# A second level of the block scheme in a graph layer's adjacency product

## The chip, the cores and the metric

One core of a Trainium2 chip runs the whole program. The metric is the time of one execution on the device in microseconds (us). TensorE (PE) multiplies matrices, VectorE (DVE), ScalarE (ACT) and GpSimd (POOL) work on elements, SyncE (SP) issues the DMAs.

## The reference

Two residual graph layers over 16 batches of 1024 nodes with 512 features, all in f32:

```python
h = jnp.maximum(_layernorm(x), 0.0)
y = jnp.einsum('nm,bmd->bnd', adj, h)
x = x + jnp.einsum('bnd,do->bno', y, weight) + bias          # layer 0
h = jnp.maximum(_layernorm(x), 0.0)
x = x + gnn_attention(h, W, a, beta, adj)                    # layer 1
```

Layer 1 forms logits from `h`, multiplies them by `adj`, takes a softmax over the nodes, multiplies it by `h W`, adds `beta` times `h W`, and applies ELU.

## The kernel before

**Products.** Every product of matrices is cut in two by two blocks and done with seven block products instead of eight (the Strassen scheme in Winograd's form). The table `PRODUCTS` names them in order: p1, p2, p6, p5, p7, p3, p4. The left factor's blocks are A11, A12, A21, A22 and the sums S1 to S4, the right factor's B11 to B22 and T1 to T4. Four blocks of sums C11, C12, C21, C22 and again S1, S2, S4 come out, since they are at once the left factor of the next product.

**Layer 0, one batch.** `layer0_a` multiplies the transposed `h` by the transposed adjacency (A in what follows); `layer0_b` multiplies the result by the weight (B). A block product of A is two halves p of 128 features, each of four matmuls over k (K 128, 512 moving columns), in one PSUM bank. Banks are named by kind: Y is shared by p1, p6, p7 and p4 and accumulates over them, X by p5 and p3, W is p2's. After each half, ACT copies the bank out or DVE adds it to a C block, which takes the partial sum before the next product accumulates in the same bank. A block product of B is two halves q of four matmuls with 256 columns; after each, DVE adds the bank to the residual tile `xr` (`done` in `layer0_b`).

**Work beside it.** `products_a` and `products_b` call `after(n)` behind each half, so that a batch has 14 numbered steps in A and 14 in B. Plans, which are dictionaries from step to calls, say what is issued there. Every engine runs its instructions in the order in which they are recorded. In A of batch b lie the rest of batch b-1 (`plan_out`): the store `keep` of `xr` to DRAM, its layer norm statistics (`bn_stats` and `bn_aggr` on DVE, then the power -0.5 on POOL), the Relu on ACT into tiles `u` of their own, two passes for the attention logits on DVE for each chunk of 128 nodes (`logits`), sums of `u` for layer 1 (`sums`) and their stores (`store`); the loads of the residual x into `xr` (`load_res`, four DMAs for each of the four tiles) and, on them, the bias (`add_bias`; POOL, on DVE for the first batch). Also there and in B lies the layer norm of batch b+1 (`plan_norm_a`, `plan_norm_b`: `load_x`, `h_stats`, `h_relu`, `h_sums`). The first softmax of layer 1 lies beside the last batch (`FIRST_A`, `FIRST_B`).

```python
for p in range(2):                      # products_a, one block product
    for k in range(HC):
        pe.matmul(ps, a_blk(an, k)[:, ts(p, P)], b_blk(bn, k), ...)
    ...                                 # read by ACT or DVE
    after(2 * n + p)
```

**Buffers.** Pool `xp` has four tiles, one for each `xr`; `up` has seven, `b4` twelve, `b2` five, PSUM eight banks.

All instructions are recorded through the helper `InOrder`, so the profile gives line 109 for all of them; they are told apart by tile names (`y_` for A, `po_` for B of layer 0, `z_` and `pq_` in layer 1).

Of the kernel before, what the change touches and what calls it, by code (L numbers as in the profile page):

```python
# [59 lines left out]
def kernel(  # L60
# [57 lines left out]

    def products_a(name, a_blk, b_blk, after):


        c = new_c(name)
        s = {}
        banks = {}
        for n, (prod, an, bn, kind, first, last) in enumerate(PRODUCTS):
            for p in range(2):
                if first:
                    banks[kind, p] = bank(f"{name}_{kind}{p}")
                ps = banks[kind, p]
                for k in range(HC):  # L130
                    pe.matmul(
                        ps, a_blk(an, k)[:, ts(p, P)], b_blk(bn, k),
                        start=(first and k == 0), stop=(last and k == HC - 1),
                        skip_group_check=True,
                    )
                c11, c12, c21, c22 = (c[k][:, p, :] for k in ("C11", "C12", "C21", "C22"))
                if prod == "p1":
                    act.copy(c11, ps)
                elif prod == "p2":
                    add(c11, ps, c11)  # L140
                elif prod == "p6":
                    act.copy(c12, ps)
                elif prod == "p5":
                    act.copy(c22, ps)
                elif prod == "p7":
                    add(c22, ps, c22)
                elif prod == "p3":
                    if not s:
                        for k in ("S1", "S2", "S4"):
                            s[k] = b4.tile([P, 2, 512], F32, tag="b4", name=f"{name}_{k}")  # L150
                    s1, s2 = s["S1"][:, p, :], s["S2"][:, p, :]
                    add(c12, ps, c12)
                    add(s1, c12, c22)
                    add(s2, s1, c11, ALU.subtract)
                    add(c12, c11, c12, ALU.subtract)
                else:
                    act.copy(c21, ps)
                    add(s["S4"][:, p, :], c21, s["S2"][:, p, :], ALU.subtract)
                after(2 * n + p)
        return {  # L160
            "A11": c["C11"], "A12": c["C21"], "S3": c["C12"], "A22": c["C22"],
            "S1": s["S1"], "S2": s["S2"], "S4": s["S4"],
        }
# [47 lines left out]

    def inv_std(r, nb, mv):

        k = r.shape[1]
        pool.tensor_scalar(r, mv[:, :, 1], EPS, 1.0, op0=ALU.add, op1=ALU.mult)
        pool.tensor_tensor(r, r, half[:, 0:k], op=ALU.pow)
        pool.tensor_scalar(nb, mv[:, :, 0], -1.0, 1.0, op0=ALU.mult, op1=ALU.mult)
        pool.tensor_tensor(nb, nb, r, op=ALU.mult)
# [6 lines left out]
    class Norm:  # L225


        def __init__(self, name, src, dst):
            self.name, self.src, self.dst = name, src, dst
            self.n = src.shape[1]  # L230

        def stats(self):
            mv = stat.tile([P, self.n, 2], F32, tag="mv", name=f"mv_{self.name}")
            for k in range(self.n):
                stats(mv[:, k, :], self.src[:, k, :])
            self.r = stat.tile([P, self.n], F32, tag="r", name=f"r_{self.name}", bufs=3)
            self.nb = stat.tile([P, self.n], F32, tag="nb", name=f"nb_{self.name}", bufs=3)
            inv_std(self.r, self.nb, mv)

        def relu(self, c=slice(None)):  # L240
            for k in range(self.n):
                act.activation(
                    self.dst[:, k, c], self.src[:, k, c], AF.Relu,
                    scale=self.r[:, k : k + 1], bias=self.nb[:, k : k + 1],
                )

# [14 lines left out]
    def h_stats(b, k):  # L261

        if k % 2 == 0:
            hs[b, k // 2] = b8.tile([P, HC, D], F32, tag="b8", name=f"h_{b}_{k // 2}")
        dst = hs[b, k // 2][:, ts(k % 2, 2), :]
        h_norms[b, k] = Norm(f"h{b}_{k}", xs.pop((b, k)), dst)
        h_norms[b, k].stats()
# [4 lines left out]
    def left_half(k, a11, a12, a21, a22, s):  # L272

        s1, s2, s4 = (s[n][:, ts(k, 2), :] for n in ("S1", "S2", "S4"))
        add(s1, a21, a22)
        add(s2, s1, a11, ALU.subtract)
        add(a21, a11, a21, ALU.subtract)
        add(s4, a12, s2, ALU.subtract)
# [41 lines left out]
    def add_bias(b, nh, q):  # L320

        t = xrs[b, nh, q]
        bias = bias_bc[:, None, :].to_broadcast([P, 2, D])
        (pool if b else dve).tensor_tensor(t, t, bias, op=ALU.add)
# [18 lines left out]
    class LayerOut:  # L343
# [18 lines left out]
        def stats(self, nh, q):  # L362
            xr = xrs.pop((self.b, nh, q))
# [5 lines left out]
            self.us[nh, q] = up.tile([P, 2, D], F32, tag="up", name=f"u_{self.b}_{nh}_{q}")  # L369
            self.norms[nh, q] = Norm(f"u{self.b}_{nh}_{q}", xr, self.us[nh, q])  # L370
            self.norms[nh, q].stats()

        def relu(self, nh, q):
            self.norms[nh, q].relu()

        def logits(self, nh, q):
            junk = self.s["S1"].rearrange("p k d -> p (k d)")[:, 0:D]
            for k in range(2):
                self.logit_parts(4 * nh + 2 * q + k, self.us[nh, q][:, k, :], junk, v_bcs)
# [8 lines left out]
        def sums(self, q):  # L388
            u1, u2 = self.us[0, q], self.us[1, q]
            left_half(q, u1[:, :, 0:HD], u2[:, :, 0:HD], u1[:, :, HD:D], u2[:, :, HD:D], self.s)  # L390
# [382 lines left out]
    def logit_weights(k):  # L773

        v = stat.tile([P, DC], F32, tag="v", name=f"v_{k}")
        junk = up.tile([P, D], F32, tag="up", name=f"junk_{k}")
        for dc in range(DC):
            dve.tensor_tensor_reduce(
                out=junk, in0=w1_t[:, dc, :], in1=v_bcs[k], scale=1.0, scalar=0.0,
# [34 lines left out]
    def plan_first():  # L814
# [4 lines left out]
            12: [(add_bias, 0, 0, 0)], 13: [(add_bias, 0, 0, 1)],  # L819
        }  # L820

    def plan_out(o, b):

        plan = {
            -1: [(o.keep, 0, 0), (o.stats, 0, 0), (o.keep, 0, 1), (o.stats, 0, 1)],
            0: [(o.relu, 0, 0), (o.keep, 1, 0), (o.stats, 1, 0)],
            1: [(o.relu, 0, 1), (o.keep, 1, 1), (o.stats, 1, 1)],
            2: [(o.relu, 1, 0)], 3: [(o.relu, 1, 1)],
        }

        for i, (nh, q) in enumerate(halves):
            plan.setdefault((4 if b == 1 else 2) + i, []).append((o.logits, nh, q))
        for q in range(2):
            plan.setdefault((8 if b == 1 else 6) + q, []).extend([(o.sums, q), (o.store, q)])
        for i, (nh, q) in enumerate(halves):
            plan.setdefault(3 + i, []).append((load_res, b, nh, q))
            plan.setdefault(6 + i, []).append((add_bias, b, nh, q))
        return plan

    def plan_norm_a(b):  # L840
        return {
            8: [(h_stats, b, 0), (h_stats, b, 1)],
            9: [(h_relu, b, 0), (h_relu, b, 1), (load_x, b, 2), (load_x, b, 3)],
            12: [(h_stats, b, 2)], 13: [(h_stats, b, 3), (h_relu, b, 2)],
        }

    def plan_norm_b(b):
        plan = {0: [(h_relu, b, 3)], 2: [(h_sums, b, 0)], 5: [(h_sums, b, 1)]}
        if b + 1 < B:
            plan[7] = [(load_x, b + 1, 0), (load_x, b + 1, 1)]  # L850
        return plan

    def plan_softmax(order, s):
# [33 lines left out]
        -1: "R0 R1 R2 R3", 2: "B E0", 3: "E1 R4", 4: "E2 R5", 5: "E3 R6 S", 6: "b E4 R7",  # L887
        7: "E5", 8: "E6", 9: "E7 s", 10: "D", 12: "T1a", 13: "T1b",
    }
    FIRST_B = {0: "d", 1: "T2a", 2: "T2b", 4: "T3a", 5: "T3b"}  # L890
# [3 lines left out]
    sms = [Softmax(b) for b in range(B)]  # L894
    for b in range(B):
        plans = [plan_first() if b == 0 else plan_out(LayerOut(b - 1), b)]
        if b + 1 < B:
            plans.append(plan_norm_a(b + 1))
            if b == 1:
                plans.append({2: [(logit_weights_back, 0), (logit_weights_back, 1)]})  # L900
            plan_b = merged(plan_norm_b(b + 1), plan_softmax(EARLY_B.get(b, {}), sms[0]))
            if b == 0:
                plan_b = merged(
                    {2: [(add_bias, 0, 1, 0), (add_bias, 0, 1, 1)]}, plan_b,
                    {9: [(logit_weights, 0)], 11: [(logit_weights, 1)]},
                )
        else:
            plans.insert(0, plan_softmax(FIRST_A, sms[0]))
            plans.append({
                8: [(load_u, 0, ("U00", "U01"))],  # L910
                10: [(load_u, 0, ("U10", "U11", "S2", "S1", "S4"))],
            })
            plan_b = merged(plan_softmax(FIRST_B, sms[0]), plan_softmax(LOGITS_B, sms[1]))
        if 0 < b <= G:
            plans.append({13: [(store_mask, b - 1)]})
        layer0_a(b, merged(*plans))
        layer0_b(b, plan_b)
# [69 lines left out]
```

## Time and profile before

| | |
|---|---|
| median of 8 runs | 2361.21 us (2357.83 to 2363.21) |
| the profiled execution | 2359.86 us, its span 2358.0 us |
| granted TensorE clock, mean | 0.997 |
| ACT busy in layer 1, 1200 to 1400 us | 135.5 us |
| ACT busy in layer 0, 600 to 800 us | 52.9 us |
| HBM | 251.92 MB read, 133.50 MB written |

The span runs from the first to the last instruction; the execution's own time has 1.9 us more around it. A busy time is the time in which an engine had an instruction under way. In a group's line stand the operation, the tile written and those read, the shapes and the count; then the total time, the mean of one in ns, and the idle time of the engine before them with what ended it. In a timeline's line stand start and length, and in brackets the idle time before.

### The profile page before, as it was taken

The page shows a single profiled execution, that of the slowest core. Times are in us where ns is not written, and L with a number is a line of the kernel's source. Part 1 is how long each engine was busy: PE and PEld are TensorE (multiplying, and loading weights), DVE is VectorE, ACT ScalarE, POOL GpSimd, SP SyncE. Part 2 cuts the span into 40 slices and gives each one's busy share as a digit, 9 for nine tenths or more (in the row PEclk, how much of TensorE's full clock was granted, in tenths as well). Part 3 has the DMA queues.
Part 4 walks back from the last instruction along what each step waited for, and adds up shares of the span by engine and source line. Part 5 has one row for each costly group of instructions (what it writes and reads, how often), then busy time and mean ns, then how long its engine had stood idle before and what let it go on. Part 6 is the DMA issues. An engine that isn't in the chain of part 4 may idle for free.

```text
span 2358.0 us, 26003 instructions
## 1 busy us (share of the span) xinstructions
PE 2334.3 (99%) x7264; PEld 1373.6 (58%) x7264; DVE 1862.7 (79%) x3950; ACT 1071.3 (45%) x2675; POOL 560.1 (24%) x732
## 2 busy tenths in 40 slices
PE   9999999999999999999999999999999999999998
PEld 5655556665566655666555666556665566655665
DVE  5888877788788888787968787877877778777774
ACT  3212212212222232222356776667766677666743
POOL 1223323223322233232102221122211222102220
PEclk9999999999999999999999999999999999999999
DMA  6444434434346445345554556555565554555541
GB/s 219 108 152 152 167 119 152 161 128 158 137 134 206 160 162 180 105 145 184 195 189 152 165 186 202 188 166 172 185 216 172 182 164 157 183 174 172 170 129 46
DMA packets 207234, 382.99 MB, mean 162 GB/s; under 512 B 80240, under 2 KB 88432, under 8 KB 207088
## 3 DMA queue, kind: packets, MB, share of 16 engines
q1 hardware_dynamic: 206768, 380.81, 49.0%
q8 instruction: 57, 0.93, 0.2%
q14 instruction: 89, 0.73, 0.1%
q10 hardware_dynamic: 320, 0.52, 0.1%
HBM read 251.92 MB, written 133.50 MB: 163 GB/s over the span
## 4 chain that ended last, share of the span: by engine, by line
PE 78%; DVE 7%; DMA 6%; ACT 5%; SPq 2%; issue 2%; POOL 0%; DVEq 0%; ACTq 0%
PE y_Y L109 17%; PE z_Y L109 13%; PE po_Y L109 9%; PE y_X L109 8%; PE pq_Y L109 6%; PE z_X L109 6%; PE po_X L109 5%; PE y_W L109 4%; PE z_W L109 4%; PE pq_X L109 3%; DMA md<-mx 2%; ACT e L109 2%; PE po_W L109 2%; PE pq_W L109 2%; DVE e L109 2%; SPq L109 2%
## 5 line engine op out<-in xcount | busy, mean ns | idle before, releaser
L109 POOL TENSOR_TENSOR x<-x,r 128x512 f32<-128x512 f32 x120 | 226.2, 1896 | 895.9 <-DVE x L109 486.2
L109 ACT ACTIVATE e<-e,nm 128x256 f32<-128x256 f32 x480 | 237.4, 498 | 159.6 <-DVE nm L109 159.6
L109 ACT COPY y_C<-y_Y 128x512 f32<-128x512 f32 x96 | 56.2, 586 | 547.0 <-PE y_Y L109 538.7
L109 DVE CUSTOM_DVE_ANT_0 e<-e,mask 128x256 f32<-128x256 f32 x512 | 234.4, 509 | 70.6 <-DMA mask<-maskd 37.6
L109 DVE CUSTOM_DVE_ANT_0 uS<-u,v_bc 128x512 f32<-128x512 f32 x240 | 241.8, 1008 | 19.5 <-DMA v_bc<-vd 3.1
L109 PE MATMUL y_Y<-adjT_B,h 128*128 128x512 f32 x512 | 226.7, 596 | 1.9 <-ACT adjT_B L109 1.9
L109 PE MATMUL z_Y<-pT,ul_U 128*128 128x512 f32 x512 | 224.9, 592 | 0.0
L109 ACT ACTIVATE e<-s2b,s1b 128x256 f32<-128x256 f32 x512 | 214.7, 506 | 16.5 <-DMA s2b<-s2d 16.5
L109 DVE STREAM_TRANSPOSE pT<-e 128x512 f32<-128x512 f32 x240 | 155.6, 686 | 70.6 <-ACT e L109 70.6
L109 ACT ACTIVATE h<-x,nb_h,r_h 128x512 f32<-128x512 f32 (+1 forms) x132 | 98.4, 793 | 219.3 <-POOL nb_h L109 219.1
L109 PE MATMUL pq_Y<-w_c,z_C 128*128 128x256 f32 x768 | 176.3, 381 | 1.7 <-DVE z L109 0.9
L109 PE MATMUL po_Y<-w_c,y_C 128*128 128x256 f32 x768 | 173.6, 379 | 0.0
L109 POOL TENSOR_TENSOR xr<-xr,bias_bc 128x1024 f32<-128x1024 f32 x60 | 151.6, 2535 | 66.0 <-DMA xr<-in_x_dram 49.4
L109 PEld LDWEIGHTS y_Y<-adjT_B,h 128*128 128x128 f32 x512 | 97.8, 191 | 118.8 <-issue 115.4
L109 PEld LDWEIGHTS z_Y<-pT,ul_U 128*128 128x128 f32 x512 | 97.3, 190 | 115.6 <-issue 111.9
L109 PEld LDWEIGHTS pq_Y<-w_c,z_C 128*128 128x128 f32 x768 | 144.4, 190 | 33.2 <-issue 7.7
L109 PEld LDWEIGHTS po_Y<-w_c,y_C 128*128 128x128 f32 x768 | 145.9, 190 | 26.7 <-issue 7.7
L109 ACT ACTIVATE r<-z,rs 128x256 f32<-128x256 f32 x192 | 95.7, 499 | 110.0 <-DVE z L109 110.0
L109 DVE TENSOR_TENSOR xr<-po_Y,xr 128x512 f32<-128x512 f32 x128 | 86.6, 687 | 55.2 <-PE po_Y L109 55.0
L109 PE MATMUL po_X<-w_c,y_S 128*128 128x256 f32 x512 | 115.7, 379 | 0.0
L109 PE MATMUL pq_X<-w_c,z_S 128*128 128x256 f32 x512 | 115.6, 379 | 0.0
L109 PE MATMUL z_Y<-pT_T,ul_U 128*128 128x512 f32 x256 | 112.5, 592 | 0.0
(127 smaller groups left out, 4164.9 us busy)
## 6 DMA issues: line engine op xcount, KB each, us to landing
mask<-maskd SPq DMA_DIRECT2D x128, 512.0 KB
x<-in_x_dram SPq DMA_DIRECT2D x64, 512.0 KB
xr<-in_x_dram SPq DMA_DIRECT2D x256, 128.0 KB
x1d<-xr SPq DMA_DIRECT2D x64, 512.0 KB
ul_U<-ud_U SPq DMA_DIRECT2D x64, 512.0 KB
x<-x1d SPq DMA_DIRECT2D x64, 512.0 KB
out_dram<-x SPq DMA_DIRECT2D x252, 128.0 KB
ud_U<-u SPq DMA_DIRECT2D x60, 512.0 KB
```

The source lines that it names most:

```text
L109: return lambda *args, **kwargs: tc.keep_in_program_order(f(*args, **kwargs))
```

## The change

For batches 1 to 15, A is done by `products_a2`. There p1, p5 and p3 are cut once more: the 256 by 512 left block and the 512 by 512 right block into two by two blocks, with seven inner products r1 to r7 of two matmuls each (128 stationary columns, 256 moving). r1, r6 and r7 accumulate in a bank y of their own; r1's value is copied out by ACT before r6 accumulates, r6's is read by DVE before r7 does. r4 and r2, r3 go to the halves of the product's two banks. DVE then adds the copied values to these banks in PSUM. The inner product steps alternate with the plain matmuls of p2, p6 and p7; p4 comes last. A has 25 numbered steps.

- `inner_right` makes the inner right sums of B11, T1 and B22 once, in batch 0, in place and in tiles `ext`, which take four tiles of `up` and one of `b2`. `inner_left` makes the left ones in each batch, four DVE adds for each product.
- The layer norm statistics of x for batches 1 to 15 and of `u` go from DVE to ACT, one chunk of 512 features at a call (`Norm.sums`): a pass with the total, a one-element operation for the mean, a pass with the squares.
- Relu writes `u` over `xr`. `load_res` of the next batch therefore waits for the store of `u`.
- `add_bias` is always on POOL, in halves of 256 columns, and lies in steps 0 to 7 of B.
- Logits, sums and statistics are issued by chunk or by pair of adds, at steps of their own. The chunks of the first `u` tile and one of the second lie in B. Steps in the first batch, whose A stays as it was, are scaled from 25 to 14. The softmax beside the last batch is spread further, into B.

```diff
     def products_a(name, a_blk, b_blk, after):
...
+    def products_a2(name, a_blk, b_blk, inner, after):
...
+            lefts = {
+                "r1": left[:, 0:2, P : 2 * P], "r2": left[:, 2:4, P : 2 * P],
+                "r7": left[:, 0:2, 0:P], "r4": left[:, 2:4, 0:P], "r5": sums[:, 0],
+                "r6": sums[:, 1], "r3": sums[:, 2],
+            }
...
+            outs = {
+                "r1": (y, True), "r4": (i0[:, 0:256], first), "r5": (x, not first),
+                "r6": (y, False), "r7": (y, False), "r2": (i1[:, 0:256], first),
+                "r3": (i1[:, 256:512], False),
+            }
+            def step(r):
+                o, start = outs[r]
+                for k in range(2):
                     pe.matmul(
+                        o, lefts[r][:, k, :], rights[r][:, k, :], start=(start and k == 0),
+                        stop=(k == 1), skip_group_check=True,
                     )
+                if r == "r1":
+                    act.copy(t[:, 0, :], y)
+                elif r == "r5":
+                    act.copy(t5, x)
+                elif r == "r6":
+                    add(t[:, 1, :], y, t5)
+                elif r == "r7":
+                    act.copy(t[:, 2, :], y)
+                    if first:
+                        i0v = i0.rearrange("p (a n) -> p a n", a=2)
+                        add(i0v, i0v, t[:, 2:3, :].to_broadcast([P, 2, 256]))
+                    else:
+                        add(t[:, 3, :], y, t5)
+                        add(i0, i0, t[:, 2:4, :].rearrange("p a n -> p (a n)"))
+                elif r == "r3":
+                    add(i1, i1, t[:, 0:2, :].rearrange("p a n -> p (a n)"))
+
+            return [partial(step, r) for r in ("r1", "r4", "r5", "r6", "r7", "r2", "r3")]
...
+        k = 0
+        for two, one in (("p1", "p2"), ("p5", "p6"), ("p3", "p7")):
+            inn, pla = inner_steps(two), plain_steps(one)
+            for m in range(7):
+                inn[m]()
+                pla[m if m < 4 else m + 1]()
+                if m == 3:
+                    pla[4]()
+                    if one != "p2":
+                        reads(one, 0)
+                elif m == 4:
+                    reads(two, 0)
+                    if one == "p2":
+                        reads(one, 0)
+                elif m == 6:
+                    for prod in (two, one) if one == "p2" else (one, two):
+                        reads(prod, 1)
+                after(k + m)
+            k += 7
...
+        def sums(self, k):
...
+            act.activation(junk, self.src[:, k, :], AF.Identity, accum_out=total)
+            act.activation(mean, total, AF.Copy, scale=-1.0 / D)
+            act.activation(junk, self.src[:, k, :], AF.Square, bias=mean, accum_out=var)
...
-        bias = bias_bc[:, None, :].to_broadcast([P, 2, D])
-        (pool if b else dve).tensor_tensor(t, t, bias, op=ALU.add)
+    def add_bias(b, nh, q, oh):
+
+        t = xrs[b, nh, q][:, :, ts(oh, HD)]
+        bias = bias_bc[:, None, ts(oh, HD)].to_broadcast([P, 2, HD])
+        pool.tensor_tensor(t, t, bias, op=ALU.add)
...
+        late = 4 if b == 1 else 0
+        return steps(
+            (-1, o.keep, 0, 1), (-1, o.keep, 1, 0), (-1, o.keep, 1, 1), (-1, o.stats, 0, 1, 1),
+            (0, o.stats, 1, 0, 0), (1, o.relu, 0, 0), (2, o.stats, 1, 0, 1),
+            (3, o.stats, 1, 1, 0), (4, o.relu, 1, 0), (5, o.stats, 1, 1, 1), (6, o.relu, 0, 1),
+            (8, o.relu, 1, 1),
+            (3 + late, o.logits, 0, 0, 0), (5 + late, o.logits, 0, 0, 1),
+            (7 + late, o.logits, 1, 0, 0), (8 + late, o.logits, 1, 0, 1),
+            (9 + late, o.sums, 0, 0), (10 + late, o.sums, 0, 1), (10 + late, o.store, 0),
+            (11 + late, o.logits, 0, 1, 0), (12 + late, o.logits, 0, 1, 1),
+            (12 + late, load_res, b, 0, 0), (13 + late, load_res, b, 1, 0),
+            (13 + late, o.logits, 1, 1, 0), (15 + late, o.logits, 1, 1, 1),
+            (16 + late, o.sums, 1, 0), (17 + late, o.sums, 1, 1), (17 + late, o.store, 1),
+            (19 + late, load_res, b, 0, 1), (20 + late, load_res, b, 1, 1),
+        )
...
+            (9, h_stats, b, 0, 0), (10, h_stats, b, 0, 1), (12, h_stats, b, 1, 0),
+            (13, h_stats, b, 1, 1), (14, h_relu, b, 0), (15, load_x, b, 2), (16, h_relu, b, 1),
+            (17, load_x, b, 3),
...
+                    (11, out_of.stats, 0, 0, 0), (12, out_of.stats, 0, 0, 1),
+                    (13, out_of.stats, 0, 1, 0), (12, out_of.keep, 0, 0),
```

## Prediction

> **What bounds the kernel now.** I read the page's engine shares first, then busy time in stretches, then the chain of waits in order of time, then groups by shape and the timelines of DVE, ACT, POOL and SP in one batch. All instructions carry L109, a recording helper, so I go by tiles.
>
> ```profile
> span 2358.0 us, 26003 instructions
> PE 2334.3 (99%) x7264; PEld 1373.6 (58%) x7264; DVE 1862.7 (79%) x3950; ACT 1071.3 (45%) x2675; POOL 560.1 (24%) x732
> ```
>
> PE is busy all the time. The two stretches below are one layer 0 batch: adjacency product (A), then weight product (B). Columns: length, then busy us of PE, PEld, DVE, ACT, POOL, granted clock, DMA share, GB/s.
>
> ```profile
> 532.00:580.10 48.10, 48.10 (x114) 21.47 (x113) 42.43 (x82) 12.89 (x19) 18.28 (x29) 1.00 0.48 164
> 580.10:604.30 24.20, 24.20 (x113) 21.13 (x112) 16.67 (x29) 3.62 (x5) 3.08 (x8) 1.00 0.25 88
> ```
>
> PE has no gap; DVE is 88% busy in A, ACT 27%. The chain of waits there is PE alone:
>
> ```profile
> 539.26 6.87 PE y_W L109 x16
> 580.46 3.45 PE po_Y L109 x16
> ```
>
> A product of A (8 matmuls, two records each) is 6.87 us, 0.859 per 512-column matmul; one of B (8 matmuls of 256 columns) is 3.45, 0.432 each. So time can be won only by taking matmul columns away, and lost by making PE wait.
>
> **What PE loses.** In 15 of 16 batches p1, p5 and p3 become seven inner products of two 256-column matmuls: 14 x 0.432 = 6.04 us for 6.87, so 0.83 a product, 45 x 0.83 = **37 us**. A falls from 48.1 to 45.6 us. Weight loads are nearly hidden at this shape already (PEld 21.1 of 24.2 in B).
>
> **What it asks of DVE in A.** A 512-element add is 0.69 us and a 1024-element one 1.22, so a 256-element one is about 0.42. New: 8 inner left sums and 4 inner adds (12 x 0.42 = 5.0) and 6 adds that read and write PSUM. No row writes PSUM from DVE; the nearest reads it (`xr<-po_Y`, 0.69), bounds 0.6 and 1.2, I take 0.69: 4.1. Kept: 14 reads of products at 0.66 = 9.2, 16 logit passes at 1.58 a pair = 12.6, 8 `u` sums = 5.3, small 0.4. Sum 36.6 of 45.6. Gone: 12 normalization statistics at 0.66 + 0.18, and the collisions with POOL's bias:
>
> ```profile
> 545.51 5.49 POOL L109 TENSOR_TENSOR xr<-xr,bias_bc 128x1024 f32<-128x1024 f32 x2 [0.68 <-DMA xr<-in_x_dram]
> 546.20 2.60 DVE L109 CUSTOM_DVE_ANT_0 uS<-u,v_bc 128x512 f32<-128x512 f32 x1
> 548.84 2.71 DVE L109 CUSTOM_DVE_ANT_0 uS<-u,v_bc 128x512 f32<-128x512 f32 x1
> ```
>
> A logit pass of 0.69 takes 2.6 beside a bias add; four bias adds a batch hold DVE about 8 us.
>
> **What it asks of ACT.** A chunk's statistics become three activations. The rows:
>
> ```profile
> L109 ACT ACTIVATE er<-er,nm 128x256 f32<-128x256 f32 x32 | 15.8, 499 | 2.4 <-DMA er<-ed 2.4
> L109 ACT ACTIVATION_READ_ACCUMULATOR e<-e,nm 128x1 f32 x480 | 91.2, 190 | 0.0
> L109 ACT ACTIVATE h<-x,nb_h,r_h 128x256 f32<-128x256 f32 x8 | 4.3, 594 | 2.5 <-POOL nb_h L109 2.5
> L109 ACT ACTIVATE h<-x,nb_h,r_h 128x512 f32<-128x512 f32 x124 | 94.2, 806 | 216.8 <-POOL nb_h L109 216.6
> ```
>
> 256 more elements cost 806 - 594 = 212 ns, a second per-partition operand 594 - 499 = 95. So the total pass (no such operand) is 499 - 95 + 212 = 0.62, the squares (one) 0.71, the one-element mean 0.19; consecutive accumulating passes start one duration apart, but the mean waits for the read-out, about 0.1, and two handoffs add 0.08: **1.7 us a chunk**. No row shows that dependent chain: without the waits 1.5, with every read-out and handoff in full 2.0. In A: 9 chunks 15.3, 6 pairs of Relu at 1.52 = 9.1, 8 copies of 0.59 = 4.7, 9 half copies at 0.37 = 3.3: 32.4 of 45.6. Neither engine is full; what counts is who is late in its queue.
>
> **Where PE can now wait.** Inner r6 accumulates where ACT must first have copied r1; r7 accumulates where DVE must first have added r6 and the ACT copy of r5. From r6's end to r7 lie only two plain matmuls, 1.72 us, of which 0.2 to reach DVE, 0.42 for the add and 0.15 back leave 0.95 for queueing. I lay the queues out from A's start, a step being 1.72 us (that with r6 2.58). ACT can begin the chunks of u(0,0) when DVE has finished its xr, 20.3 us into the B before, 3.9 ahead of A; that one and u(0,1) are four chunks of 1.7. First group: so ACT does them to 2.9, r1's copy to 3.3 (wanted 5.2), a chunk, two Relus, r5's copy at 6.8; DVE adds to 7.3, r7 is due 7.75: no wait. Then ACT: two chunks to 10.1, r7's copy, DVE's correction to 11.3, the read of C11 to 12.05, two Relus, a chunk to 15.2, the second read of C11 to 15.8. DVE, in order behind that read, adds W1 to 16.55, then four logit passes to 19.75 and two sums to 21.0, and only then r6's add of p5, to 21.4. r7 is due 20.65: PE waits **0.9 us**. Third group: the add is done at 33.3, r7 due 34.45: none. With 2.0 a chunk the same walk gives 1.1 + 0.75 + 1.2 = 3.05 us a batch, with 1.5 about 0.1. I take 0.9, the value of the rows: 15 x 0.9 = 13.5 us.
>
> **Moves with one answer.** The bias goes to B as eight halves (POOL's undisturbed add of 512, `x<-x,r` at 1340.82, takes 1.32): 10.6 us of POOL beside B's first half. DVE's adds there read PSUM; two of them, `z<-pq_Y` at 1395.01, take 1.28 together while POOL has an add under way, so I charge nothing. The bound above: each bias half holds DVE its 1.32 us; DVE's B (14 adds, 8 h sums, 4 inner sums) is 17 of 24.2, so 10.6 more would run some 3 us over, 45 us in all. In layer 0's first batch bias and statistics leave DVE and twelve right sums of 0.69 come, under 6.87 us products: hidden, 0 to 3. The Trainium skill, "GPSIMD Engine Reference", section "Key points", says that GpSimd contends with VectorE where the latter has two SBUF inputs. By that rule these adds go free; the trace has only the few rows above to say so.
>
> **Transfers.** U now overwrites xr in place, so the next residual waits for U's store. SP's order late in A: five stores and two small ones (before: 567.46 to 574.45, 7.0 us), one x load (3.1), then xr(0,1) (2.9), landing 2.4 later. The sums end at 35.7, so it lands near 51, 4.5 us into B; POOL's and DVE's next work waits there, and r_h and the Relu of the next h behind POOL. Y1 is wanted again 8.6 into B: hidden, 3.4 us to spare. In batch 1 everything is four steps later, 6.9 us: PE waits 2 to 4, I take 3 (0 to 6). In batch 15 softmax steps move into B: 1 (0 to 5).
>
> **Sum.** 2359.9 (the profiled execution, 1.3 under the median 2361.2) - 37.1 + 13.5 + 4 = 2340.3; on the median **2342**.
>
> **Rivals.** *ACT sets the pace*: at 2.0 a chunk the stalls take 46 us: 2361 - 37 + 46 + 4 = 2374, slower; it turns at 33 / 15 = 2.2 us of stall a batch, near 1.9 a chunk. For: no row for the chain, and a Relu pair of 1.52 sits before urgent copies. Against: 32 of 46 us of load. *No stall*: with 1.5 a chunk or earlier reads, 2324 to 2330. *Residuals late*: if stores go at the 3.1 us of an x load rather than 1.2, xr(0,1) lands 9 us later and PE waits 5 a batch: near 2410. Against: the 7.0 us above. *The clock*: the stretch of before with the most short gaps kept its clock, so I charge nothing:
>
> ```profile
> 1400.00:1600.00 200.00, 198.23 (x582) 109.70 (x581) 156.82 (x386) 139.32 (x402) 41.87 (x30) 1.00 0.55 177
> ```
>
> A rule speaks against it: the skill's "TensorE: Matmul & The Clock Gate", section "A second HAM failure mode: psum-queue depth-cycling", has PE idling briefly between bank groups and its clock swinging down to half. The page's window is 3.4 us; one such window a batch would be an estimated 15 x 1.7 = 26 us, 2368 in all.
>
> **How the numbers follow.** A measurement here tells about 0.2% (4.7 us) from no change. Forecast with 0.3 to 1.8 of stall: 2330 to 2356, 0.43. No stall: 0.16. Stall between, 2356 to 2366: 0.12, of which 0.02 still faster. ACT pace, 2366 to 2380: 0.22. Late residuals: 0.07. Faster 0.61, same 0.10, slower 0.29. The range 2326 to 2376 leaves out some 0.04 below and 0.12 above.
>
> **What would show it.** Right: y products of 256 columns at 0.43 us, A near 46.5 with one PE gap of about 1 us before p5's r7, ended by DVE; ACT chunks at 1.7; bn gone from u and h; logit passes at 0.69; B still 24.2. Wrong: gaps before r6 ended by ACT in every group (ACT pace), gaps in B ended by DVE xr (residuals), a granted clock under 1 in layer 0, or a time above 2356.

## The result and the profile after

The changed kernel takes 2372.35 us (median of 12 runs) against 2361.07 for the kernel before (median of 33); the ratio is 1.0049 (1.0041 to 1.0057). The profiled execution took 2374.73. It is slower by about half a per cent, where 2342 was forecast.

The page of the changed kernel, span and engine shares:

```profile
span 2373.0 us, 28070 instructions
PE 2314.9 (98%) x7804; PEld 1479.8 (62%) x7804; DVE 1730.4 (73%) x3808; ACT 1506.1 (63%) x4010; POOL 564.2 (24%) x680
```

PE's busy time fell by 19.4 us (2334.3 to 2314.9), yet the span grew by 15.0: PE now waits, and part of its busy time is at half clock. One steady batch, A and then B, in busy time by stretches (length, then PE, PEld, DVE, ACT, POOL, granted clock, DMA share, GB/s):

```profile
539.60:585.90 46.30, 45.84 (x149) 27.96 (x148) 34.85 (x78) 31.46 (x78) 9.46 (x20) 1.00 0.48 166
585.90:610.10 24.20, 24.20 (x114) 21.28 (x112) 14.59 (x23) 13.99 (x36) 10.95 (x14) 1.00 0.32 97
```

This batch is what the forecast describes: A is 46.3 us instead of 48.1, with one gap of 0.46. Where the time went is seen in PE's timeline, which gives start, length and, in brackets, the idle time before with what ended it. The first row is the steady gap, the others are of batches 1, 10 and 15:

```profile
560.88 1.13 PE L109 MATMUL y_p5y<-adjT_T,hS 128*128 128x256 f32 x4 [0.46 <-DVE y_p5t L109]
111.51 2.08 PE L109 MATMUL y_p1y<-adjT_B,h 128*128 128x256 f32 x4 [11.71 <-DVE y_p1t L109]
764.18 2.07 PE L109 MATMUL y_p1y<-adjT_B,h 128*128 128x256 f32 x4 [3.65 <-DVE y_p1t L109]
1144.12 2.08 PE L109 MATMUL y_p5y<-adjT_T,hS 128*128 128x256 f32 x4 [4.42 <-DVE y_p5t L109]
```

The rows name VectorE, but the two of p1 only pass a wait on. The add of r6 needs ScalarE's copy of r5, and that copy stands behind a Relu. ScalarE's and VectorE's timelines in batch 1, then ScalarE's in batch 10:

```profile
109.23 1.52 ACT L109 ACTIVATE xr<-xr,nb_u,r_u 128x512 f32<-128x512 f32 x2 [10.63 <-DMA x1d<-xr]
110.65 0.35 ACT L109 COPY in_p<-y_Y 128x256 f32<-128x256 f32 x1
111.03 0.42 DVE L109 TENSOR_TENSOR y_p1t<-y_p1y,in_p 128x256 f32<-128x256 f32 x1 [9.79 <-ACT in_p L109]
...
761.90 1.52 ACT L109 ACTIVATE xr<-xr,nb_u,r_u 128x512 f32<-128x512 f32 x2 [2.56 <-DMA x1d<-xr]
```

The Relu overwrites `xr`, so it waits until the store of `xr` to `x1d` has read it. In batch 10 that store goes out late because SyncE's queue holds two things ahead of it, the second of which waits for the first to land (SyncE's timeline):

```profile
754.92 0.42 SPq L109 DMA_DIRECT2D md<-mx  x1
757.37 1.74 SPq L109 DMA_DIRECT2D mall<-md  x4
759.21 2.92 SPq L109 DMA_DIRECT2D x1d<-xr  x4
```

In batch 1 the store is issued at 92.72 beside the two `vd` stores (92.26 and 97.74) and ScalarE's wait for it ends only at 109.23. From 84 to 116 us the trace counts 1117 packets under 512 B, and in several slices of 0.8 us in this stretch the DMA engines are nine tenths busy at 20 to 50 GB/s; `vd` is scattered in elements of 4 bytes.

The clock, in stretches of 4 us: in the gap of batch 1, after it, after the gap of batch 10, and after a gap of 0.98 us in batch 9:

```profile
104.00:108.00 4.00, 0.00 (x0) 0.00 (x0) 0.00 (x0) 0.00 (x0) 0.00 (x0) 0.52 1.36 57
112.00:116.00 4.00, 4.00 (x11) 2.58 (x11) 0.70 (x1) 3.09 (x9) 1.08 (x3) 0.70 0.83 256
764.00:768.00 4.00, 3.82 (x7) 2.42 (x8) 1.89 (x6) 3.31 (x11) 1.08 (x3) 0.50 0.32 125
692.00:696.00 4.00, 4.00 (x16) 2.73 (x15) 2.33 (x5) 3.23 (x7) 0.14 (x1) 1.00 0.00 0
```

**The account.** Lengths of A and B are taken from the first matmul of each in PE's timeline. Fifteen steady batches would give 15 x (48.07 - 46.32) = 26.3 us. Against it stand, over 46.32: A of batch 1 14.1, of batch 10 6.1, of batch 12 5.5, of batch 15 6.6, of batches 2, 9, 11, 13 and 14 together 4.8 (gaps of p1 up to 0.98 us); and B of batch 1 is 2.7 longer than before. Together 39.8, so layer 1 starts 13.5 us later than before (1196.7 against 1183.2). Layer 1's own length was 1171 to 1178 us over all kernels below without a pattern, so the start of layer 1 is the steadier measure.

### The profile page after: what moved, and what is told of

Same layout as the page of the kernel before. It is cut to its first block, busy times and chain, and to the rows that moved or that the text cites. A ratio compares the mean times of both kernels' runs of the same rounds, so it can differ in the third digit from the quotient of the medians.

```text
span 2373.0 us, 28070 instructions
## 1 busy us (share of the span) xinstructions
PE 2314.9 (98%) x7804; PEld 1479.8 (62%) x7804; DVE 1730.4 (73%) x3808; ACT 1506.1 (63%) x4010; POOL 564.2 (24%) x680
## 4 chain that ended last, share of the span: by engine, by line
PE 30%; ACT 6%; DVE 6%; DMA 6%; issue 2%; SPq 2%; POOL 0%; DVEq 0%; ACTq 0%
PE z_Y L109 12%; PE z_X L109 6%; PE pq_Y L109 4%; PE z_W L109 3%; ACT e L109 3%; DMA md<-mx 2%; DVE e L109 2%; PE pq_X L109 2%; SPq L109 2%; PE pq_W L109 1%; ACT z L109 1%; DMA sd<-sm 1%; ACT r L109 1%; DMA mask<-maskd 1%; DVE x L109 1%
## 5 line engine op out<-in xcount | busy, mean ns | idle before, releaser
L109 POOL TENSOR_TENSOR xr<-xr,bias_bc 128x512 f32<-128x512 f32 x128 | 162.5, 1291 | 287.5 <-DMA xr<-in_x_dram 203.7
L109 DVE CUSTOM_DVE_ANT_0 uS<-xr,v_bc 128x512 f32<-128x512 f32 x240 | 167.2, 697 | 5.7
L109 ACT ACTIVATE junk<-xr 128x512 f32<-128x512 f32 x120 | 75.3, 628 | 129.8 <-issue 118.6
L109 PE MATMUL y_Y<-adjT_B,h 128*128 128x512 f32 (+1 forms) x332 | 152.3, 563 | 1.6 <-ACT adjT_B L109 1.6
L109 PE MATMUL y_W<-adjT_B,h 128*128 128x512 f32 x256 | 129.4, 602 | 0.0
L109 PE MATMUL y_Y<-adjT_T,hS 128*128 128x512 f32 x256 | 128.0, 596 | 0.0
```

The lines of the kernel that those rows point to most:

```text
L109: return lambda *args, **kwargs: tc.keep_in_program_order(f(*args, **kwargs))
```

## The experiments

The theory at this point: the matmul columns are won as forecast, and lost again because ScalarE's in-place Relu carries the lateness of a store into the inner products. The rivals: ScalarE's own load sets the pace; the second level or the moved work loses by itself. Every kernel is the changed kernel with the edit shown. All figures in one table (us; A1 is A of batch 1, and so on; L1 is the start of layer 1):

| kernel | median | ratio to before | A1 | B1 | A10 | A15 | B15 | L1 |
|---|---|---|---|---|---|---|---|---|
| before | 2361.1 | 1 | 48.1 | 32.0 | 48.1 | 48.1 | 25.0 | 1183.2 |
| changed | 2372.4 | 1.0041 to 1.0057 | 60.4 | 34.7 | 52.4 | 52.9 | 25.0 | 1196.7 |
| e1_vd | 2361.7 | 0.9999 to 1.0018 | 46.0 | 32.5 | 51.3 | 52.9 | 25.2 | 1186.6 |
| e2_x | 2363.7 | 1.0001 to 1.0030 | 60.3 | 32.0 | 47.7 | 52.9 | 25.0 | 1186.0 |
| e3_exp | 2376.6 | 1.0051 to 1.0089 | 60.4 | 32.3 | 51.2 | 53.7 | 25.7 | 1196.2 |
| e4_relu | 2361.0 | 0.9985 to 1.0013 | 59.1 | 32.3 | 48.4 | 52.9 | 25.5 | 1185.1 |
| e5_combo | 2342.5 | 0.9912 to 0.9937 | 51.5 | 24.2 | 47.5 | 52.2 | 26.9 | 1166.9 |
| e6_one | 2363.6 | 1.0006 to 1.0026 | 55.1 | 30.9 | 48.1 | 48.1 | 24.2 | 1187.5 |
| e7_one_combo | 2356.3 | 0.9977 to 0.9998 | 48.1 | 24.2 | 48.1 | 48.1 | 24.2 | 1174.6 |
| e8_b15 | 2378.4 | 1.0064 to 1.0090 | 60.7 | 32.3 | 51.2 | 51.2 | 34.8 | 1204.4 |
| e9_a0 | 2336.9 | 0.9880 to 0.9926 | 46.1 | 24.2 | 47.5 | 52.2 | 26.5 | 1159.2 |
| e10_both | 2334.4 | 0.9880 to 0.9928 | 46.1 | 24.2 | 47.5 | 51.3 | 24.2 | 1157.0 |
| e11_nobias | 2330.5 | 0.9863 to 0.9905 | 46.0 | 24.2 | 47.4 | 52.9 | 24.4 | 1156.1 |
| e12_bn | 2349.8 | 0.9950 to 0.9974 | 49.7 | 24.2 | 48.4 | 52.1 | 26.8 | 1174.1 |

Each part's length is from one profile. Steady parts repeat within hundredths, but parts with a long gap do not: A10 is 52.4 in the changed kernel and 51.2 to 51.3 in e1, e3 and e8, whose batch 10 is the same, and B1 is 34.7 against 32.0 to 32.3 in e2, e3 and e8, whose first batches are the same (there A2 is 49.1 instead of 47.4).

In the plans' strings `X` and `x` are the exchange of the maxima of the softmax (a store `md` and four loads `mall`), `M` the masked maxima, `R` reloads a block of logits (`er<-ed`), `E` takes its exponential on ScalarE and then a pair of transposes on VectorE.

**e1_vd: the small stores out of the way.**

```diff
-                1: [(inner_right, "p3")], 10: [(logit_weights, 0)], 12: [(logit_weights, 1)],
+                1: [(inner_right, "p3")], 2: [(logit_weights, 0)], 4: [(logit_weights, 1)],
```

> The two logit weight steps of the first batch go from steps 10 and 12 to steps 2 and 4 of its B; nothing else changes. Theory (the in-place Relu makes ACT wait for the x1d store, which the 4-byte vd stores slow): ACT waits no more than 1 us for x1d(0,0), PE's gap of 11.7 us in batch 1 falls under 1 us, A of batch 1 goes from 60.4 to 46 to 48 us with its clock back at 1.00, time 2372.4 - 13 = 2359 (2356 to 2362). Rival (ACT's own load holds r5's copy): the gap stays within 2 us of 11.7, time 2370 to 2373. Rival (x1d is slow for another reason, such as the other loads at that moment): a gap of 4 us or more remains, time 2364 to 2370.

Batch 1's gap of 11.7 us is gone and A1 is 46.0. The time is 2.7 us over the centre of the expectation, mainly because the moved VectorE passes made a gap of their own in the first batch's B, 5.7 us with the clock's fall. VectorE's timeline there, then PE's:

```profile
78.59 0.69 DVE L109 TENSOR_TENSOR xr<-po_W,xr 128x512 f32<-128x512 f32 x1
79.79 0.75 DVE L109 CUSTOM_DVE_ANT_0 junk<-w_t,v_bc 128x512 f32<-128x512 f32 x1
80.59 1.63 DVE L109 CUSTOM_DVE_ANT_0 junk<-w_t,v_bc 128x512 f32<-128x512 f32 x1
82.26 1.63 DVE L109 CUSTOM_DVE_ANT_0 junk<-w_t,v_bc 128x512 f32<-128x512 f32 x1
86.22 3.06 PE L109 MATMUL po_Y<-w_c,y_C 128*128 128x256 f32 x8 [3.71 <-DVE xr L109]
```

Beside the bias halves on GpSimd most of these passes take 1.63 instead of about 0.7, while the add that reads PSUM keeps its 0.69.

**e2_x: the exchange of maxima out of the way.**

```diff
-        9: {4: "e2", 8: "M2 K2 e3", 11: "M3 K3 X"}, 10: {4: "e4", ...
-        11: {4: "e6", 8: "M6 K6 e7", 11: "M7 K7 x"}, 13: {9: "N n"},
+        9: {4: "e2", 8: "M2 K2 e3", 11: "M3 K3"}, 10: {2: "X", 4: "e4", ...
+        11: {4: "e6", 8: "M6 K6 e7", 11: "M7 K7"}, 12: {2: "x"}, 13: {9: "N n"},
```

> The two spread_max steps beside batches 9 and 11 (store md, four loads that wait for it, all on SP's queue ahead of x1d's store) go to step 2 of the next batch's B. Theory: x1d is issued 2.5 to 4 us earlier in batches 10 and 12, ACT's wait for it goes, PE's gaps of 3.65 and 4.14 us fall to 1 us or less, the two A parts go from 52.4 and 51.8 to 46.3 to 47.8, time 2372.4 - 10 = 2362 (2360 to 2364). Rival (ACT's own load): both A parts stay within 1 us of 52, time 2371 to 2373.

As the theory has it. The same store and the same Relu of batch 10, with no wait in brackets (SyncE's timeline, then ScalarE's):

```profile
753.01 3.69 SPq L109 DMA_DIRECT2D x1d<-xr  x4
757.26 1.50 ACT L109 ACTIVATE xr<-xr,nb_u,r_u 128x512 f32<-128x512 f32 x2
```

**e4_relu: the copy taken out from behind the wait.** SyncE's order stays; only the Relu moves.

```diff
-            (0, o.stats, 1, 0, 0), (1, o.relu, 0, 0), (2, o.stats, 1, 0, 1),
+            (0, o.stats, 1, 0, 0), (3, o.relu, 0, 0), (2, o.stats, 1, 0, 1),
```

> Relu of the first u tile goes from step 1 to step 3, so it stands behind the copies of r5 on ACT; SP's queue and all DMAs stay. Theory (the wait for x1d hurts only because r5's copy stands behind it): x1d lands as late as before, yet PE's gaps in batches 10 and 12 shrink from 3.65 and 4.14 to under 1.5 us, and in batch 1 from 11.7 to 3 to 9 us, since there the Relu then holds ACT's copy of r7 and the correction behind it; time 2372.4 - 12 = 2360 (2354 to 2366); in steady batches nothing or a gain of some tenths. Rival (what is late is DVE's adds or PE's own operands, not ACT's order): gaps as they were, time 2371 to 2374.

In batches 10 and 12 the gaps before p1's r7 are gone, though the store is as late as it was; at p5 two gaps of 0.7 and 0.8 us stay. In batch 1 PE waits 1.84 us before r7, for VectorE's inner left sums, and then at the next place where ScalarE is needed, the read of a product (ScalarE's timeline, then PE's):

```profile
108.69 1.52 ACT L109 ACTIVATE xr<-xr,nb_u,r_u 128x512 f32<-128x512 f32 x2 [9.08 <-DMA x1d<-xr]
113.56 2.07 PE L109 MATMUL y_Y<-adjT_T,hS 128*128 128x512 f32 x2 [6.59 <-ACT y_C L109]
```

So both links are shown: e2 takes the lateness away and keeps the order, e4 keeps the lateness and changes the order. ScalarE's amount of work is the same in all three kernels.

**e3_exp and e8_b15: batch 15.** In e3 the four exponentials go from steps 7, 9, 12, 14 to 11, 12, 14, 18; in e8 the first four to 11, 14, 20, 22 and the rest into B.

```diff
-        -1: "R0 R1", 4: "R2 R3", 7: "B E0", 9: "E1 R4", 12: "E2", 14: "E3 R5", 15: "S b",
+        -1: "R0 R1", 4: "R2 R3", 11: "B E0", 12: "E1 R4", 14: "E2", 18: "E3 R5", 19: "S b",   # e3
+        -1: "R0 R1", 4: "R2 R3", 11: "B E0", 14: "E1 R4", 20: "E2 R5", 22: "E3", 23: "S b",   # e8
+        24: "R6 R7",                                                                          # e8
```

> In batch 15 the four exponentials that lay at steps 7, 9, 12 and 14 go to 11, 12, 14 and 18 (behind r6's add of p5; S and b from 15 to 19, the last reloads from 18 to 20). Theory (two pairs of DVE transposes of 2.6 us and the ACT exponentials stand ahead of r6's add): the gap of 4.4 us before r7 of p5 falls to 0.5 us, A of batch 15 from 52.9 to 47 to 48, its clock back at 1.00, time 2372.4 - 5.5 = 2367 (2365 to 2369). Rival (batch 15 is bound by something else, such as the load of u tiles): A stays over 51, time 2371 to 2373.

> In batch 15 the first exponentials go to steps 11, 14, 20 and 22, the fifth to the eighth into B, and the sum T3 of the softmax into layer 1's first A. Theory (VectorE has no room for four pairs of transposes between p5's r6 and p3's r6; it has some behind p3): the gaps before r7 of p5 and of p3 fall to 0.5 us or less, A of batch 15 from 52.9 to 47 to 48.5, B of it no more than 26, time 2372.4 - 5 = 2367 (2365 to 2370). Rival (batch 15 is over its VectorE load wherever the transposes stand): A and B of batch 15 together stay within 2 us of 77.8, time 2370 to 2375.

Both missed. In e3 the gap moved to p3:

```profile
1138.12 1.13 PE L109 MATMUL y_p5y<-adjT_T,hS 128*128 128x256 f32 x4 [0.47 <-DVE y_p5t L109]
1155.39 2.07 PE L109 MATMUL y_p3y<-adjT_B,hS 128*128 128x256 f32 x4 [3.56 <-DVE y_p3t L109]
```

In e8 p3 still waited 2.9 us, and in B ScalarE waited 8.3 us for a reload now issued too late (`er<-ed`), VectorE 7.9 for ScalarE and PE 7.4 for VectorE. Neither order repairs batch 15. What stands ahead of r6's add of p5 in the changed kernel (VectorE's timeline):

```profile
1138.46 1.30 DVE L109 STREAM_TRANSPOSE pT<-er 128x512 f32<-128x512 f32 x2 [1.62 <-ACT er L109]
1142.46 1.30 DVE L109 STREAM_TRANSPOSE pT<-er 128x512 f32<-128x512 f32 x2
```

Two pairs of transposes, 1.3 us each, and one wait of 1.62 us for ScalarE's exponential make the add 4 us later than in a steady batch, and PE's gap is 4.42 instead of 0.46.

**e6_one: the second level alone taken out.**

```diff
-        two_levels = b > 0
+        two_levels = False
```

(with the inner sums left out and every step of batch 15 scaled to fourteen)

> The changed kernel with the second level alone taken out, and every other place as in the changed kernel. Theory (the inner products make PE depend on ACT within 2 us, the plain ones only within a product or two of 6.87 us): the waits for x1d stay on ACT, but PE's gap is 4 us or less in batch 1 (10.6 of waiting against the slack of the banks) and none in batches 10, 12 and 15; A elsewhere 48.07, time 2362 to 2370, under the changed kernel's 2372. Rival (waiting on ACT costs plain products as much): 2380 or more.

ScalarE waits for the store as long as before, and the plain products let two thirds of it pass without a gap of PE (ScalarE's timeline, then PE's):

```profile
109.33 1.52 ACT L109 ACTIVATE xr<-xr,nb_u,r_u 128x512 f32<-128x512 f32 x2 [11.27 <-DMA x1d<-xr]
111.38 6.58 PE L109 MATMUL y_Y<-adjT_T,hS 128*128 128x512 f32 x8 [3.90 <-ACT y_C L109]
```

It is the only gap of an A part in the whole kernel: batches 10, 12 and 15 are 48.07. With the clock's fall behind it A1 is 7.0 us over a steady A, against 14.1 with the second level. What the second level gives up, then, is PE's tolerance of a late ScalarE or VectorE.

**e5_combo and e7_one_combo: four moves together, with and without the second level.** The edits of e2 and e4, the logit weights at steps 7 and 9, and

```diff
-        late = 4 if b == 1 else 0
+        late = 1 if b == 1 else 0
```

> Four moves of place together, no work added or taken: the logit weight steps of the first batch at 7 and 9 of its B, both spread_max steps in the next batch's B, Relu of the first u tile at step 3, and the residual loads of batch 1 one step late instead of four. Theory: the A parts of batches 1, 10 and 12 fall to 46.1 to 47.5 us, B of batch 1 from 34.7 to 25 to 28, A of batch 2 back to 46.3 to 47.4; the gains of the single runs add up: 2372.4 - 13 - 9 - 8 - 1 - 3 (0.2 a batch from the Relu) = 2338 (2334 to 2345), so faster than before by about 1%. Rival (what moved only changes which wait shows, as it did in the first batch's B when the weights stood at 2 and 4): 2350 to 2361.

> The four moves of the run before, but with the second level taken out (all batches by the plain seven products, no inner sums, steps scaled to fourteen); bias, statistics on ACT and the pieces stay. Theory (only the matmul columns gain; the rest of the change gains nothing since PE was without gaps): A is 48.07 in every batch, B 24.17, time 2358 to 2364, that is 20 to 26 us over the run before. Rival (the moved statistics and bias carry part of the gain): under 2352. Rival (one-level products suffer from the new places too): over 2366.

The gains add up to 2342.5, which beats both kernels. Without the second level the same moves give 2356.3: PE has no gap of an A or B part in layer 0 then, and layer 1 starts 8.6 us earlier than in the kernel before, all of it from B1 (7.8) and B15. That is a little under the 2358 to 2364 expected: the theory had PE without gaps in the kernel before and left out its 5.87 us in B1. Elsewhere the moved bias, statistics and pieces win nothing, as the theory has it. In e5 VectorE's logit weight passes at step 9 pushed the inner left sums of batch 1 back; PE waited 1.86 us for `in_p`, and the clock fell (granted 0.82 and 0.75 in the two stretches of 4 us from 94), A1 51.5.

**e9_a0 and e10_both: the best versions.** Both keep the edits of e2 and e4. e9 puts the logit weights into VectorE's idle time in the first A and makes `late` 0; e10 also rearranges batch 15 (the loads of two groups of `u` blocks move there too).

```diff
+            6: [(logit_weights, 0), (logit_weights, 1)],             # in plan_first, e9 and e10
+        late = 0                                                     # e9 and e10
...
+        -1: "R0 R1", 4: "R2 R3", 7: "B E0", 11: "E1 R4", 13: "E2 R5", 20: "E3 R6", 21: "S b R7",
+        23: "E4",                                                    # e10
+        0: "E5", 2: "E6", 4: "E7 s", 6: "D", 7: "T1a", 8: "T1b", ... # e10
```

> As the combination of four moves (2342.5), but the logit weight steps go to step 6 of the first batch's A, where VectorE is idle for 9.5 us (40.2 to 49.7), and the residual loads of batch 1 go where all other batches have them. Theory (in the combination batch 1 lost 5.4 us only because the weight steps delayed the inner left sums on VectorE): A of batch 1 falls from 51.5 to 46.1 to 46.5, A of batch 2 from 47.2 to 46.1 to 46.5, time 2342.5 - 6 = 2336 (2334 to 2339). Rival (batch 1 waits for other things of the first batch as well): A of batch 1 over 48, 2339 to 2343.

> The run before, and in batch 15 the second exponential goes from step 9 to 11 (behind r6's add of p5), the fourth from 14 to 20 and the fifth to 23, the sums' spread to 21, the diagonal to step 6 of B, the loads of U10 and U11 behind the residual loads. Theory (one pair of transposes too many stands before r6's add, and one too many before p3's): A of batch 15 from 52.2 to 47 to 48.5, B from 26.9 to 24.2 to 26, time 5 us under the run before: 2331 (2328 to 2335). Rival (VectorE's load, or late reloads, only move the gap): A and B of batch 15 together stay at 79 +- 1.5, time within 2 us of the run before.

e9 falls where it should: A1 and A2 are 46.1. Set against e7, the second level is worth 15.4 us of layer 0 (1174.6 - 1159.2). e10 wins 2.4 us in B15 and only 0.9 in A15, where gaps of 3.05 and 1.39 stay (the first batch took 1.1 more), and its ratio cannot be told from e9's. The expectation for A15 missed again: the gap of 3.05 is still before p5's r7, with only one pair of transposes and its wait of 1.62 ahead of the add. Both are about 1% faster than before.

**e11_nobias and e12_bn: two terms of the sum, on e9.** In e12 `chunk` calls `bn_stats` and `bn_aggr` for one chunk, and the power on GpSimd after the second.

```diff
-        plans_b = [plan_bias(b)]
+        plans_b = []                            # e11
...
-            h_norms[b, k].sums(c)
+            h_norms[b, k].chunk(c)              # e12
```

> The first of these kernels with all bias adds of layer 0 left out (output lacks the bias). It tells what the bias beside B costs. Theory (GpSimd's halves lie beside VectorE adds that read PSUM and cost nothing): steady A 46.1 and B 24.2 as with it, only the last batch's B up to 2.7 us shorter, time 0 to 3 us under the kernel with bias. Rival (it holds VectorE, so that it sets where the next batch's statistics and sums start): steady A falls by 0.3 us or more a batch, time 5 us or more under.

> The first of these kernels with the statistics of x for batches 1 to 15 back on VectorE (bn_stats and bn_aggr by chunk, 0.84 us each, eight a batch, 6.7 us of VectorE for 14.7 us of ScalarE); u's stay on ScalarE. Theory (neither engine is full; what counts is which one stands in front of r6 and r7): A longer by 0 to 1 us a batch, since the chunks at steps 9 and 10 stand ahead of r6's add of p5 on VectorE (0.84 more wait there), so 2336 to 2351. Rival (ScalarE's statistics are what makes the inner products wait): A falls under 46, 2330 or less.

Without the bias A is 0.13 us shorter in each steady batch and B15 2.2, and layer 1 starts 3.1 us earlier; the medians differ by 6.5, which would fit the rival, but the two intervals overlap, and the rival's 0.3 us a batch is not there. By layer 0 the bias costs 3 us in all. With the statistics back on VectorE, steady A goes from 46.14 to 46.96, and the gap is again before p5's r7:

```profile
257.25 1.13 PE L109 MATMUL y_p5y<-adjT_T,hS 128*128 128x256 f32 x4 [1.10 <-DVE y_p5t L109]
```

That is 0.82 more for one chunk of 0.84 ahead of the add. (In batch 1 the gap is 2.07 us and the clock falls, so A1 is 49.7.) ScalarE lost work and PE waited longer, which speaks against ScalarE as the pace.

## Why the prediction was wrong

**Matmul columns (37 us) and the steady stall (13.5).** Right in kind. Steady A was to be about 46.5 and is 46.32. Without its gap it is 45.86, so the columns brought 15 x 2.21 = 33; the gap is 0.46 instead of 0.9, at the place named and ended by VectorE, 6.9 us in all. The two errors nearly cancel: net 26.3 against 23.6 forecast.

**The loads.** Right: ScalarE 31.5 us of A (32.4 forecast), VectorE 34.9 (36.6), a chunk of statistics 1.84 (1.7, inside its bounds), the add of 256 elements 0.42 and the PSUM correction 0.70 (0.69).

**Where PE can now wait: the step that failed.** The walk through ScalarE's queue put "a chunk, two Relus, r5's copy at 6.8" with the Relus at their own 1.52 us and concluded "no wait" for p1. The section on transfers saw that U overwrites `xr`, but drew from it only that the next residual waits for U's store. The same overwriting makes the Relu itself wait for the store of `xr`. Before, Relu wrote tiles of its own and ScalarE never waited for that store. I did not follow where in SyncE's queue `x1d` stands in each batch. So a wait that the sum put at nothing held ScalarE for 10.63 us in batch 1 and 2.56 and 3.05 in batches 10 and 12, and PE behind it. A1, A10 and A12 are 25.7 of the 39.8 us; up to 23 of them are this wait with the clock's fall, since 1.4 and 1.6 us stay in A10 and A12 when it is gone (e2). e1, e2 and e4 show it from both sides.

**Batch 1's late residuals (+3).** Right in size: B1 and A2 together lost 3.8 us more than in the kernel before, and 2.8 to 3.1 in e2, e3 and e8. VectorE's add in B1 waits for the load of the residual:

```profile
163.22 0.69 DVE L109 TENSOR_TENSOR xr<-po_Y,xr 128x512 f32<-128x512 f32 x1 [8.21 <-DMA xr<-in_x_dram]
```

With the loads near their usual place (e5, e7, e9) B1 is 24.2, and none of the other moves alone does that (e1, e2, e4: 32.0 to 32.5), so their place is the cause. The kernel before lost its 7.8 us in B1 in another way: its residuals were loaded early (from 103.49), but VectorE waited 2.37 us (until 147.42) for the next batch's x and then did that batch's statistics ahead of the add.

**Batch 15 (+1, 0 to 5).** Mis-sized: 6.6 over a steady A, and in A instead of B. It was priced as softmax steps moved into B; what counts is that a pair of transposes (1.3 us) and VectorE's wait for the exponential before it (1.62) stand ahead of the add, against a slack estimated at 0.95 before r7. Batches 9 and 11 lose 1.4 us; there p1's r7 waits for ScalarE's copy behind a Relu without any wait for a store, probably because the `M` passes in the B before make ScalarE start late, but no run moves them. How to place batch 15 without a gap stays open.

**The clock (nothing charged).** Wrong in the changed kernel, a consequence of the long gaps. In A1, B1, A10, A12 and A15 the lengthening exceeds the gaps by 2.1, 4.7, 2.9, 1.8 and 2.6 us, 14 in all (in the kernel before 1.9, in B1). The steady batches kept 1.00 through their 0.46 us, so the estimate of one window in every batch was not met. The Trainium skill, "TensorE: Matmul & The Clock Gate", section "HAM oscillation — how this bites in real kernels", wants no PE idle gap over some 3.4 us. That agrees with the gaps of 3.65 to 11.7 us here, but is no safe line: 1.86 us was enough in e5 and 2.07 in e12, while 3.05 us in e10 left 1.00.

**Bias in B (nothing charged).** Nearly right: 3 us in all. e1 shows the other side: the skill's "GPSIMD Engine Reference", section "Key points", has GpSimd contend with VectorE where the latter has two SBUF inputs, and most passes of that kind took 1.63 instead of 0.7 beside the bias.

**The rivals.** "ScalarE sets the pace" gave 2374, two microseconds from the result, by a mechanism that was not there: no steady gap before r6 is ended by ScalarE (batch 1 alone has one, of 0.73). A time near a rival's is no proof of the rival. That the four moves then bring 2342.5, about the forecast's 2342, is partly luck: the kernel so mended also wins the 7.8 us that the kernel before lost in B1, which no term of the sum held, and it still loses some 21 us against its own steady parts (A of batches 1, 2, 9 to 12, 14 and 15, and B15).

## What to carry to other kernels

When an operation is made to write in place, list every reader of the old contents, stores included, and follow each through its queue in every batch that differs (first, last, those with extra work beside them). Cutting a product into smaller dependent ones also cuts how late a helper engine may be: here one wait of 11 us made a gap of 3.9 with plain products and of 11.7 with inner ones. Put an instruction that may wait for a DMA behind those which the matmuls need within the next 2 us.

## What the hardware showed unexpectedly

- Two stores of 2 KB in 4-byte elements lay beside four stores of 512 KB, and the first of these took over 16 us (92.72 to 109.2); with the small stores earlier the Relu could start at 101.75 without a wait (e1).
- The granted clock after a gap is no function of its length alone: 1.00 after 0.98, 1.75 (layer 1) and 3.05 us; 0.50 in the stretch of 4 us right after 3.65 and 4.42; in e9 the first matmuls after 4.24 us ran at full speed (1.13 us for four records), and then came 0.57 from 1106 to 1110.
- Nor is the length of the fall: in batch 10 the changed kernel has 0.50 for 6.83 us (762.91 to 769.74) and e3 for 3.41 (762.12 to 765.53), after gaps of 3.65 and 3.69. PE was busy for 5.56 and 3.01 us of it; half of the difference is about the 1.2 us between the two lengths of A10.
